# Inverse square roots by ScalarE's root and one Newton step, attention's loads issued by GpSimd, and a fifth float16 tile for p

## The chip, the cores and the metric

The kernel runs on one core of one Trainium2 chip. The metric is device time in microseconds (us) of one execution. The engines are TensorE (PE, matmuls; its weight loads are listed apart as PEld), VectorE (DVE), ScalarE (ACT), GpSimd (POOL) and SyncE (SP), which issues DMAs; each has its own instruction queue and works through it in order. "SPq" in a profile is the sync queue. A line number such as L810 is a line of the kernel before.

## The reference

For x of 1024 x 512, layer-normalised to xn, the output is `x + attention(xn) * silu(ffn(xn))`. Attention has 32 query heads and 8 key/value heads of width 128; q and k are normalised per head, `t * rsqrt(mean(t*t) + 1e-6) * w`, the scores get a causal mask and a bias `slope * (key position - query position)`, and after softmax and the product with v the heads go through Wo. The feed-forward network has 4-bit integer weights with a scale and a zero per group of 128, inner width 1792. Inputs and output are float32.

## The kernel before

The work runs in four stages that follow one another. **Feed-forward** (layer norm, gate and up, then down): its result, through silu, is stored to DRAM as `gd`. **Projections**: twelve, in the order kv, q, q, four times; a `Projection` object holds one. Each has eight tiles of 128 rows. In `tile` TensorE makes a tile in PSUM (four PSUM tiles rotate), ScalarE copies it to `f` and squares it with a row sum into `ss`, one column for each head. After four tiles (a half) `queue_half` puts the rest of the work into later steps of a clock that ticks once per tile: `inverse` makes `ms` on VectorE and a first guess of its inverse root by an integer shift and subtraction (`rsqrt_seed`), `newton` runs three times on GpSimd (at steps 0, 1 and 1), the last one for a q also multiplying by a scale for each head; `normalize` on GpSimd (step 2 on) multiplies `f`; `halves` on VectorE (step 4 on) splits it into two float16 halves; a DMA transposes these and another stores them to `kd` or `qd` in DRAM. Between the tiles `prepare` scales and splits the weights of the next projection: `split_head` casts to `wh` on ScalarE (L527), then VectorE makes `wl` (L528), which TensorE needs for the next projection's first tile. The last two projections run together with the first steps of attention, and the last one's finishing is spread over attention's steps.

**Attention** goes through 8 groups (a key head with its four query heads), each in four blocks of 256 query rows, each block in 4 heads x 2 row tiles: a `step` for each, 256 in all. Step n issues, for different steps of the pipeline, the scores of n (TensorE), the exponentials of n-1 (VectorE L799, ScalarE L800), the high float16 half of n-3's p (ScalarE, L810), the low half of n-4's (VectorE, L819) and the DMA transpose of both into `pT` (L820), the product with v nine steps later, and then the output projection. The pair of halves is a tile `p16`; P16_BUFS of them rotate, so L810 waits for the transpose that read the tile P16_BUFS uses before. A block's number of key columns runs from 256 to 1024, so the length of a step varies. The loads of attention (`load_keys`, `load_values`, `load_queries`, `load_wo`, and `gate_load` for the last sum) are issued by the sync queue, which also issues every transpose. `split_wo` makes a float32r pair of Wo's rows on ScalarE and GpSimd (L770), six steps ahead of use. `relative` makes the distance bias of a group from a constant tile `nrel` on GpSimd.

The order on each engine is that of the code: nothing is scheduled anew, and semaphores are put where data or buffers need them.

Of the kernel before, what the change touches and what calls it, by code (L numbers as in the profile page):

```python
# [10 lines left out]
F32 = mybir.dt.float32  # L11
# [10 lines left out]
P = 128  # L22
# [36 lines left out]
GATE_SUMS = [27, 28, 30, 31]  # L59
GATE_STEP = 2  # L60
PF_BUFS = 5
P16_BUFS = 4

_START = 2 ** (-(2 ** (-(math.log2(H) - 3))))
SLOPES = np.array([_START * _START**i for i in range(H)], dtype=np.float32)
# [5 lines left out]
def attention_gated_by_ffn_kernel(ctx, tc, x, gu_w, gu_z, gu_s, dn_w, dn_z, dn_s, wq, wkv, wo, qnw, knw, out):  # L71
# [47 lines left out]
    cs = const.tile([P, NH], F32, name="cs")  # L119
    rc = const.tile([P, 1], F32, name="rc")  # L120
    eps = const.tile([P, 3 * HKV // 2, NH], F32, name="eps")
    gsT = const.tile([P, NI, 2, KT], F32, name="gsT")

    kd = [dram.tile([P, 2, NT, 2 * HD], F16, name=f"kd{i}") for i in range(HKV // 2)]
# [339 lines left out]
    class Projection:  # L464
        def __init__(self, k, kind, i):
            self.k, self.kind, self.i, self.name = k, kind, i, f"{kind}{i}"
            self.n = NH if kind == "q" else 2
            self.f, self.ss, self.inv = {}, {}, {}

        def load(self, j):  # L470
            if j == 0:
                self.raw = wide.tile([P, KT, 512], F32, tag="wide", name=f"w{self.name}")
            sp.dma_start(self.raw[:, j], (wq if self.kind == "q" else wkv)[self.i, :, j])
# [13 lines left out]
        def norms(self):  # L487

            n = self.n
            pn = spare(self.k, f"n2_ps{self.k}")  # L490
            te.matmul(pn[:, 256 : 256 + n], lhsT=ones_bf, rhs=self.sb[:, :n], start=True, stop=True)
            if self.kind == "kv":
                for j in range(KT):
                    te.matmul(pn[:, :256], lhsT=ones_bf, rhs=self.sq[:, j, :], start=j == 0, stop=j == KT - 1)
            self.am = wp.tile([P, NH], F32, tag="am", name=f"am_{self.name}", bufs=2)[:, :n]
            ve.tensor_scalar(self.am, pn[:, 256 : 256 + n], 1.0 / W_SCALE**2, 1e-30, ALU.mult, ALU.max)
            rsqrt_seed(self.am, self.am)
            self.eps = eps[:, self.k, :n]
# [37 lines left out]
        def tile(self, t):  # L536
            n, half, r = self.n, t // HT, t % HT
            if r == 0:
                self.f[half] = fq.tile([P, HT, n, HD], F32, tag="f", name=f"f_{self.name}_{half}", bufs=3)
                self.ss[half] = fq.tile([P, HT, n], F32, tag="ss", name=f"ss_{self.name}_{half}", bufs=3)  # L540
                self.jk = wp.tile([P, NH, HD], BF16, tag="jk", name=f"jk_{self.name}_{half}")
            ps = ps1("o" if t % 2 else "m", f"ps_{self.name}_{t}")
            rows = slice(t * P, (t + 1) * P)
            for j in range(KT):
                mm3(ps, (xth[:, j, rows], xtl[:, j, rows]), (self.wh[:, j, :], self.wl[:, j, :]), j == 0, j == KT - 1)
            se.copy(self.f[half][:, r], ps[:, : n * HD].rearrange("p (g d) -> p g d", g=n))
            for i in range(n):
# [15 lines left out]
        def inverse(self, half):  # L563
# [156 lines left out]
    nrel = ap1.tile([P, S], F32, name="nrel", bufs=1)  # L720
    ge.iota(nrel, pattern=[[-1, S]], base=S - P, channel_multiplier=1, allow_small_or_imprecise_dtypes=True)
    ge.affine_select(nrel, nrel, pattern=[[-1, S]], compare_op=ALU.is_ge, fill=1e20, base=S - P, channel_multiplier=1)

    def queue_half(p, half):

# [20 lines left out]

    def load_keys(g):
        kT[g] = ap1.tile([P, NT, 2, P], F16, tag="kT", name=f"kT{g}")
        sp.dma_start(kT[g].rearrange("p t a k -> p t (a k)"), kd[g // 2][:, g % 2])

    def load_values(g):
        vT[g] = ap1.tile([P, NT, 2, HD], F16, tag="vT", name=f"vT{g}")
        sp.dma_start(vT[g].rearrange("p t a d -> p t (a d)"), vd[g])

    def load_queries(g, qb):
        qT[g, qb] = ap1.tile([P, NQT, 2, NH, P], F16, tag="qT", name=f"qT{g}_{qb}")
        sp.dma_start(
            qT[g, qb].rearrange("p t a g q -> p t (a g q)"), qd[g][qb * NQT : (qb + 1) * NQT].rearrange("t p c -> p t c")
        )

    def load_wo(g, i):
        wor[g, i] = late[0].tile([P, DM], F32, tag="wor", name=f"wor{g}_{i}", bufs=2)
        sp.dma_start(wor[g, i], wo[(g * NH + i) * HD : (g * NH + i + 1) * HD, :])

    def split_wo(g, i):
        woh[g, i] = late[0].tile([P, DM], F32R, tag="woh", name=f"woh{g}_{i}", bufs=5)
# [100 lines left out]
    def gate_load(b):  # L867
        g, qb = blocks[b]
        gx = fq.tile([P, 2, NQT, DM], F32, tag="f", name=f"gx{qb}", bufs=3)
        t0 = qb * NQT  # L870
        sp.dma_start(gx[:, 0], gd[t0 : t0 + NQT].rearrange("t p c -> p t c"))
        sp.dma_start(gx[:, 1], x[t0 * P : (t0 + NQT) * P, :].rearrange("(t p) c -> p t c", p=P))
        gates[b] = gx

    def gate_partial(b, i):
# [86 lines left out]
                act(w, r // 2)  # L962

    last_ps = None
    early = 0
    for k, p in enumerate(projections):
        if k == len(projections) - 3:
            load_keys(0)
            load_values(0)
            load_queries(*blocks[0])  # L970
            relative(0)
        for t in range(NT):
            prepare(k + 1, t)
            if t == NT - 1:
# [58 lines left out]
```

## Time and profile before

| | |
|---|---|
| median of 3 runs | 1084.39 us (1084.32 to 1085.37) |
| the profiled execution's own time | 1091.69 us |
| its span, first to last instruction | 1089.9 us |
| mean granted TensorE clock | 0.984 |
| PE busy | 1026.4 us, 94% |
| DVE busy | 887.6 us, 81% |
| ACT busy | 792.0 us, 73% |
| POOL busy | 415.9 us, 38% |
| DMA q1 (all DMAs of the sync queue) | 196.93 MB, 82.6% of 16 engines' span |

A line of the view of waits reads: engine, operand and line that waited, "<-" who ended the wait, us in total, times, longest. The chain of waits is followed back from the last instruction, at each step to what released it; its pieces are given as start, length, and what it was. The share of the DMA engines is a mean over 16. A busy TensorE is not TensorE at its peak, since matmuls overlap.

### The profile page before, as it was taken

What the parts mean: (1) busy time and instruction counts of PE and PEld (TensorE: products, weight loads), DVE (VectorE), ACT (ScalarE), POOL (GpSimd) and SP (SyncE); (2) the same over time, 40 slices, a digit from 0 to 9 for tenths busy, and PEclk for the clock granted to TensorE, in tenths of its full rate; (3) what the DMA queues carried; (4) which work ended last, traced back from release to release, by engine and by line L of the source; (5) the groups of instructions that cost most, each with busy time, mean ns of one, the idle gap of its engine ahead of it and who ended that gap; (6) DMA issues with size and microseconds to landing.
All of it is one profiled execution on the core that took longest, in us unless ns stands there. A gap on an engine that the chain in (4) does not pass through costs nothing.

```text
span 1089.9 us, 18604 instructions
## 1 busy us (share of the span) xinstructions
PE 1026.4 (94%) x5912; PEld 622.4 (57%) x5912; DVE 887.6 (81%) x1746; ACT 792.0 (73%) x2123; POOL 415.9 (38%) x551
## 2 busy tenths in 40 slices
PE   7899899999999898997999999999998999999986
PEld 4444378744444343445666666666665566666664
DVE  7888987448878888886898896998897878969974
ACT  5777633568786786787887796896886878868961
POOL 1588663137877878641105013023040030132222
PEclk8999999999999999998999999999999999999998
DMA  6123155237989999999989999998998999999993
GB/s 198 47 98 125 60 160 141 89 106 164 226 219 208 241 200 259 228 189 212 213 187 199 197 206 187 202 210 183 198 203 182 196 205 176 203 222 206 235 203 88
DMA packets 445888, 198.11 MB, mean 182 GB/s; under 512 B 394402, under 2 KB 403934, under 8 KB 445790
## 3 DMA queue, kind: packets, MB, share of 16 engines
q1 hardware_dynamic: 445790, 196.93, 82.6%
q8 instruction: 46, 0.75, 0.3%
q14 instruction: 52, 0.43, 0.2%
HBM read 71.03 MB, written 29.36 MB: 92 GB/s over the span
## 4 chain that ended last, share of the span: by engine, by line
PE 59%; DMA 13%; DVE 11%; ACT 8%; issue 5%; POOL 3%; SPq 1%; DVEq 0%; ACTq 0%; POOLq 0%
DMA pT<-p 12%; PE gu_ps L252 6%; PE av L108 4%; PE s L108 4%; PE s L109 4%; PE s L110 4%; PE av L109 4%; PE av L110 4%; PE ps_q L109 3%; PE ps_q L110 3%; PE op L110 3%; PE op L108 3%; PE ps_q L108 3%; PE op L109 3%; PE dn_ps L110 2%
## 5 line engine op out<-in xcount | busy, mean ns | idle before, releaser
L819 DVE SCALAR_TENSOR_TENSOR p<-pf,row,p 128x1024 f16<-128x1024 f32 (+7 forms) x256 | 216.6, 846 | 76.9 <-ACT p L810 74.8
L810 ACT ACTIVATE p<-pf,row 128x1024 f16<-128x1024 f32 (+7 forms) x256 | 197.0, 770 | 73.7 <-DMA pT<-p 70.2
L800 ACT ACTIVATE pf<-pf,row 128x1024 f32<-128x1024 f32 (+7 forms) x256 | 197.2, 770 | 38.5 <-DVE row L799 36.7
L770 POOL TENSOR_TENSOR wol<-wor,woh 128x512 fp32r<-128x512 f32 x32 | 59.8, 1870 | 429.5 <-ACT woh L769 373.6
L799 DVE CUSTOM_DVE_ANT_0 pf<-s,trel,cs 128x1024 f32<-128x1024 f32 (+7 forms) x256 | 207.5, 810 | 4.1 <-PE s L110 4.0
L108 PE MATMUL av<-pT,vT 128*128 128x256 f16 (+1 forms) x640 | 171.7, 268 | 25.2 <-DMA pT<-p 24.8
L109 PE MATMUL av<-pT,vT 128*128 128x256 f16 (+1 forms) x640 | 169.2, 264 | 0.0
L110 PE MATMUL av<-pT,vT 128*128 128x256 f16 (+1 forms) x640 | 169.0, 264 | 0.0
L108 PE MATMUL s<-kT,qT 128*128 128x512 f16 (+3 forms) x384 | 125.5, 327 | 6.6 <-DVE row L799 6.2
L109 PE MATMUL s<-kT,qT 128*128 128x512 f16 (+3 forms) x384 | 125.4, 327 | 0.0
L110 PE MATMUL s<-kT,qT 128*128 128x512 f16 (+3 forms) x384 | 123.8, 327 | 0.0
L108 PEld LDWEIGHTS <-vT 128*128 128x128 f16 x640 | 62.5, 98 | 106.9 <-issue 84.8
L108 PE MATMUL op<-woh,oh 128*128 128x512 f32 x248 | 121.7, 491 | 0.0
L109 PE MATMUL ps_q<-wl_q,xth 128*128 128x512 f16 x256 | 98.2, 383 | 6.7 <-DVE wl_q L528 6.7
L110 PE MATMUL op<-woh,ol 128*128 128x512 f32 x248 | 99.1, 400 | 0.0
L110 PE MATMUL ps_q<-wh_q,xtl 128*128 128x512 f16 x256 | 98.3, 384 | 0.0
L109 PE MATMUL op<-wol,oh 128*128 128x512 f32 x248 | 97.9, 395 | 0.4 <-POOL wol L770 0.4
L108 PE MATMUL ps_q<-wh_q,xth 128*128 128x512 f16 x256 | 98.2, 384 | 0.0
L847 ACT ACTIVATE oh<-av,rv 128x256 fp32r<-128x256 f32 x128 | 58.9, 460 | 24.9 <-PE av L110 24.4
L853 DVE SCALAR_TENSOR_TENSOR ol<-av,rv,oh 128x256 fp32r<-128x256 f32 x128 | 61.3, 479 | 13.6 <-ACT oh L847 13.5
L597 POOL TENSOR_TENSOR f_q<-f_q,inv_q 128x512 f32<-128x512 f32 x64 | 71.2, 1132 | 1.4
L109 PEld LDWEIGHTS <-vT 128*128 128x128 f16 x640 | 63.7, 100 | 12.2 <-issue 2.7
(179 smaller groups left out, 2315.1 us busy)
## 6 DMA issues: line engine op xcount, KB each, us to landing
qd<-tr_q SPq DMA_DIRECT2D x64, 256.0 KB, 3.6
qT<-qd SPq DMA_DIRECT2D x32, 512.0 KB, 4.4
wq<-in_wq SPq DMA_DIRECT2D x32, 256.0 KB, 3.9
wor<-in_wo SPq DMA_DIRECT2D x32, 256.0 KB, 3.7
gui<-in_gu_w SPq DMA_DIRECT2D x13, 512.0 KB, 3.6
wkv<-in_wkv SPq DMA_DIRECT2D x16, 256.0 KB, 3.8
vd<-v SPq DMA_DIRECT2D x8, 512.0 KB, 4.1
kd<-tr_kv SPq DMA_DIRECT2D x32, 128.0 KB, 2.5
```

The source lines that it names most:

```text
L108: te.matmul(ps, lhsT=lh, rhs=rh, start=first, stop=False)
L109: te.matmul(ps, lhsT=lh, rhs=rl, start=False, stop=False)
L110: te.matmul(ps, lhsT=ll, rhs=rh, start=False, stop=last)
L252: te.matmul(banks[j][:, k, :], lhsT=w[:, j, ws], rhs=x[:, j, k * 512 : k * 512 + 512], start=x is xth, stop=x is xtl)
L597: ge.tensor_tensor(f, f, ib, ALU.mult)
L770: ge.tensor_tensor(wol[g, i], raw, woh[g, i].bitcast(F32), ALU.subtract)
L799: ve.tensor_tensor_reduce(p, ps, trel[g][:, S - w :], cs[:, hh : hh + 1], 3e38, ALU.add, ALU.min, least[:, c])
L800: se.activation(p, p, AF.Exp, bias=least[:, c], scale=-1.0, accum_out=total[:, c])
L810: se.activation(p16[u, qt][:, :, 0, :], pf[u, qt], AF.Copy, scale=scale[:, qt : qt + 1])
L819: ve.scalar_tensor_tensor(lo, p, scale, hi, ALU.mult, ALU.subtract)
L847: se.activation(oh, av_ps[u], AF.Copy, scale=rv[:, g : g + 1])
L853: ve.scalar_tensor_tensor(ol, av_ps.pop(u), rv[:, g : g + 1], oh.bitcast(F32), ALU.mult, ALU.subtract)
```

## The change

Four edits:

- For the first ten projections the first guess and three Newton steps become ScalarE's square root of `ms` (at step 0, behind the next tile's squares in ScalarE's queue), a reciprocal on VectorE and one Newton step on GpSimd (both at step 1). The last two keep the guess and three steps. The q scale of each head is put into the squares instead (an immediate of the activation, and `steep` times `eps`), so the last Newton step has no form of its own.
- The loads of attention, 88 DMAs, are issued by GpSimd in place of the sync queue (the diff shows kT's; vT, qT, wor and the two of `gate_load` change in the same way).
- `p16` has five tiles in place of four.
- The constant `nrel` is gone: the first group's bias is made in its own tile, ahead of the projections, and each later one is scaled from the one before.

```diff
-P16_BUFS = 4
+P16_BUFS = 5
...
+    steep = const.tile([P, NH], F32, name="steep")
+    for i in range(NH):
+        ve.memset(steep[:, i : i + 1], (STEEPER[i] / Q_SCALE) ** 2)
...
+            self.by_root = k < 3 * HKV // 2 - 2
...
             ve.scalar_tensor_tensor(self.eps, self.am, 1e-6 * X_SCALE**2, self.am, ALU.mult, ALU.mult)
+            if self.kind == "q":
+                ve.tensor_tensor(self.eps, self.eps, steep, ALU.mult)
...
-                se.activation(self.jk[:, i], ps[:, i * HD : (i + 1) * HD], AF.Square, accum_out=self.ss[half][:, r, i : i + 1])
+                se.activation(
+                    self.jk[:, i],
+                    ps[:, i * HD : (i + 1) * HD],
+                    AF.Square,
+                    scale=STEEPER[i] / Q_SCALE if self.kind == "q" else 1.0,
+                    accum_out=self.ss[half][:, r, i : i + 1],
+                )
...
-            rsqrt_seed(a, y)
             self.inv[half] = (y, a, w)
-
-        def newton(self, half, last):
+            if self.by_root:
+                se.activation(y, a, AF.Sqrt)
+            else:
+                rsqrt_seed(a, y)
+
+        def newton(self, half, first):
             y, a, w = self.inv[half]
+            if first and self.by_root:
+                ve.reciprocal(y, y)
             ge.tensor_tensor(w, a, y, ALU.mult)
             ge.tensor_tensor(w, w, y, ALU.mult)
-            if last and self.kind == "q":
-                for i in range(NH):
-                    c = Q_SCALE / STEEPER[i]
-                    wi = w.rearrange("p (t g) -> p g t", g=NH)[:, i]
-                    ge.tensor_scalar(wi, wi, -0.5 * c, 1.5 * c, ALU.mult, ALU.add)
-            else:
-                ge.tensor_scalar(w, w, -0.5, 1.5, ALU.mult, ALU.add)
+            ge.tensor_scalar(w, w, -0.5, 1.5, ALU.mult, ALU.add)
             ge.tensor_tensor(y, y, w, ALU.mult)
...
-        for i in range(3):
-            due((i + 1) // 2, 0, lambda i=i: p.newton(half, i == 2))
+        if p.by_root:
+            due(1, 0, lambda: p.newton(half, True))
+        else:
+            for i in range(3):
+                due((i + 1) // 2, 0, lambda i=i: p.newton(half, i == 0))
...
-        sp.dma_start(kT[g].rearrange("p t a k -> p t (a k)"), kd[g // 2][:, g % 2])
+        ge.dma_start(kT[g].rearrange("p t a k -> p t (a k)"), kd[g // 2][:, g % 2])
...
-        trel[g] = ap1.tile([P, S], F32, tag="trel", name=f"trel{g}")
-        ge.tensor_scalar(trel[g], nrel, rc, float(SLOPES[g * NH + NH - 1]), ALU.mult, ALU.mult)
+        rel = trel[g] = ap1.tile([P, S], F32, tag="trel", name=f"trel{g}")
+        if g == 0:
+            ge.iota(rel, pattern=[[-1, S]], base=S - P, channel_multiplier=1, allow_small_or_imprecise_dtypes=True)
+            ge.affine_select(rel, rel, pattern=[[-1, S]], compare_op=ALU.is_ge, fill=1e20, base=S - P, channel_multiplier=1)
+            ge.tensor_scalar(rel, rel, rc, float(SLOPES[NH - 1]), ALU.mult, ALU.mult)
+        else:
+            ge.tensor_scalar(rel, trel[g - 1], float(SLOPES[g * NH + NH - 1] / SLOPES[g * NH - 1]), None, ALU.mult)
...
     last_ps = None
+    relative(0)
```

More of the change, by code (lines that the diff above doesn't have):

```diff
@@ L719, in attention_gated_by_ffn_kernel @@
     ap1 = ctx.enter_context(tc.tile_pool(name="attn1", bufs=2, side="right"))
-    nrel = ap1.tile([P, S], F32, name="nrel", bufs=1)
-    ge.iota(nrel, pattern=[[-1, S]], base=S - P, channel_multiplier=1, allow_small_or_imprecise_dtypes=True)
-    ge.affine_select(nrel, nrel, pattern=[[-1, S]], compare_op=ALU.is_ge, fill=1e20, base=S - P, channel_multiplier=1)
     def queue_half(p, half):
@@ L748, in load_keys @@
         kT[g] = ap1.tile([P, NT, 2, P], F16, tag="kT", name=f"kT{g}")
-        sp.dma_start(kT[g].rearrange("p t a k -> p t (a k)"), kd[g // 2][:, g % 2])
+        ge.dma_start(kT[g].rearrange("p t a k -> p t (a k)"), kd[g // 2][:, g % 2])
     def load_values(g):
         vT[g] = ap1.tile([P, NT, 2, HD], F16, tag="vT", name=f"vT{g}")
-        sp.dma_start(vT[g].rearrange("p t a d -> p t (a d)"), vd[g])
+        ge.dma_start(vT[g].rearrange("p t a d -> p t (a d)"), vd[g])
     def load_queries(g, qb):
         qT[g, qb] = ap1.tile([P, NQT, 2, NH, P], F16, tag="qT", name=f"qT{g}_{qb}")
-        sp.dma_start(
+        ge.dma_start(
             qT[g, qb].rearrange("p t a g q -> p t (a g q)"), qd[g][qb * NQT : (qb + 1) * NQT].rearrange("t p c -> p t c")
@@ L762, in load_wo @@
         wor[g, i] = late[0].tile([P, DM], F32, tag="wor", name=f"wor{g}_{i}", bufs=2)
-        sp.dma_start(wor[g, i], wo[(g * NH + i) * HD : (g * NH + i + 1) * HD, :])
+        ge.dma_start(wor[g, i], wo[(g * NH + i) * HD : (g * NH + i + 1) * HD, :])
     def split_wo(g, i):
@@ L870, in gate_load @@
         t0 = qb * NQT
-        sp.dma_start(gx[:, 0], gd[t0 : t0 + NQT].rearrange("t p c -> p t c"))
-        sp.dma_start(gx[:, 1], x[t0 * P : (t0 + NQT) * P, :].rearrange("(t p) c -> p t c", p=P))
+        ge.dma_start(gx[:, 0], gd[t0 : t0 + NQT].rearrange("t p c -> p t c"))
+        ge.dma_start(gx[:, 1], x[t0 * P : (t0 + NQT) * P, :].rearrange("(t p) c -> p t c", p=P))
         gates[b] = gx
@@ L970, in attention_gated_by_ffn_kernel @@
             load_queries(*blocks[0])
-            relative(0)
         for t in range(NT):
```

## The prediction

> **What bounds the kernel now.** I read the page's forty slices first, then busy time by stage, the waits, the chain of waits and the sync queue's own waits. In the slices each digit is a busy share in tenths.
>
> ```profile
> PE   7899899999999898997999999999998999999986
> ...
> PEclk8999999999999999998999999999999999999998
> DMA  6123155237989999999989999998998999999993
> ```
>
> TensorE is near full everywhere; the DMA engines are near full from the projections on. Stage by stage (in each line: length, busy us and instruction counts of TensorE, its weight loads, VectorE, ScalarE and GpSimd, then the granted clock, DMA share, GB/s):
>
> ```profile
> 240.00:480.00 240.00, 232.70 (x1080) 105.49 (x1078) 198.58 (x404) 181.72 (x821) 186.34 (x380) 0.99 0.94 215
> 480.00:515.00 35.00, 27.16 (x174) 17.05 (x173) 26.23 (x47) 27.15 (x69) 3.20 (x2) 0.92 1.09 214
> 515.00:1065.00 550.00, 527.04 (x3582) 358.69 (x3580) 469.44 (x1044) 436.39 (x988) 102.00 (x88) 1.00 0.99 200
> ```
>
> TensorE idles 7.3 us in the projections (240-480), 7.8 us in the hand-over (480-515) and 23.0 us in the attention proper (515-1065): 38 us within the change's reach. All else there is matmul work that the change leaves alone. Who waits (us in total, times, longest):
>
> ```profile
> ACT p L810 <- DMA pT<-p: 70.2, 53, 4.9
> ...
> PE av L108 <- DMA pT<-p: 24.8, 20, 3.4
> ...
> DVE q L609 <- POOL f_q L597: 22.4, 14, 2.9
> ...
> PE ps_q L109 <- DVE wl_q L528: 6.7, 3, 3.3
> ```
>
> Line 810 writes the float16 high half of p into one of four tiles, and waits until the transpose that read the tile four uses ago has landed. TensorE then waits for later transposes. The chain shows the loop closed (start, us, what):
>
> ```profile
> 497.29 0.74 ACT p L810
> 498.03 4.60 DMA pT<-p
> ...
> 502.65 0.94 ACT p L810
> ...
> 503.62 0.91 DVE p L819
> ...
> 505.33 5.20 DMA pT<-p
> ```
>
> In the projections GpSimd is late with the normalised q, VectorE waits behind it in order, its weight split (L528) comes late, and TensorE with it: 6.7 of the 7.3 us. The sync queue stands in front of the transposes with waits of its own for the loads' buffers:
>
> ```profile
> SPq L763 <- POOL wol L770: 12.9, 11, 2.2
> ...
> SPq L757 <- PE s L110: 4.1, 10, 0.7
> ```
>
> **What the Trainium skill says.** "DMA: Bandwidth & Descriptors", section "Issuing engines are not separate DMA queues": DMAs from any engine run on the same 16 DMA engines, and a second issuing engine saves only issue time. The DMA share of 0.99 in attention fits one shared resource; no GpSimd-issued DMA is in this trace. The same page, "Latency and other measured facts", puts the first byte at about 0.6 us from the sync queue and 1 us from GpSimd; not shown here. "SBUF — State Buffer", section "Who interferes with whom": a VectorE instruction with two SBUF inputs, or one in a two-port mode, contends with GpSimd's reads. The trace agrees: the cast at L609 takes 411 ns at its shortest and 683 on average over 64, the subtraction at L610 691 and 928; the slow ones (1.26 and 1.41 us) stand beside GpSimd's multiplies.
>
> **The change part by part.** *Newton steps.* Ten projections have 20 halves. A q half costs GpSimd now three times (438+296+344) ns, two times 389 and four times 328: 5.3 us. Afterwards one step: 438+296+344+389 = 1.5. A k half: 3 x (397+355+268+305) = 4.0, afterwards 1.3. With 12 q and 8 k halves GpSimd loses 12 x 3.8 + 8 x 2.7 = 67 of its 186 us in the stage, and the normalising starts some 3 us sooner. VectorE loses 40 seed instructions of 174 ns, gains 20 reciprocals (174 ns at L95) and a few [128,4] products: -3 us. Its excess from sharing, 64 x (683-411+928-691) ns = 33 us, should fall with GpSimd's work. ScalarE gains 20 roots (0.22 us at L93) and one table load (1.28 us there): 5.7 us on an engine that has 58 us free in the stage.
>
> The root adds a wait: ScalarE stands until VectorE has written ms (L569). Setting the end of the ScalarE group that precedes each root against the end of that ms, the 20 waits would be 0 to 5.7 us, 46 us in all, if VectorE stayed as late as it is. Behind it on ScalarE are the next tile's eviction and, in the first halves, the last weight cast (L527). Four PSUM tiles of 2.56 us each cover about 7 us of eviction; the cast has three tiles before TensorE needs it. So I cost the wait at nothing; the cover gone, it would cost what rival 2 says. VectorE, being relieved, should be less late too. I take -5 us for the stage. Bounds: +15 and -11 (all idle time, plus two stretches of 30 us granted 0.94 of the clock, 3.6 us).
>
> *The fifth tile.* 53 waits at L810 sum to 70.1 us. With a fifth tile each waits for a transpose one step earlier; steps come every 550/250 = 2.2 us. Taking 2 us off each wait leaves 11 us, taking 1.5 leaves 18: three quarters or more go. They go to TensorE's benefit only where the transpose was what TensorE lacked, and as far as the DMA engines (0.99) and VectorE (469 of 550 us) can follow. In some stalled stretches DMA share is lower (0.74, 0.74, 0.64 in the 5 us windows from 820), so there is room there: they are bound by the round trip of ScalarE, VectorE, queue and transpose (4.0 us median to landing).
>
> *Loads on GpSimd.* 88 loads (8 kT, 8 vT, 32 qT, 32 wor, 8 gx) leave the sync queue: about 0.57 us of issue each, 50 us in all, and the 12.9 + 4.1 us of waits shown, in front of transposes of 1.41 us each. Their bytes stay, so the engines' load does. On GpSimd each load passes wol's subtraction (L770) and the last projection's finishing; wol must be ready six steps ahead, kT, vT and qT are asked for several steps early. GpSimd is busy 102 of 550 us, so 88 loads at 1 us (my estimate from the skill's first-byte figure; bounds 0.57, as on the sync queue, and 4) are covered. If one delays a wol, TensorE waits as it did once (0.4 us): 8 places, at most 4 us. The last projection's eight normalisations (two in every fourth block of attention) stand behind a load, with two steps of slack. The iota moves, work unchanged: it waits for freed memory while GpSimd is idle (18.6 us). The memsets precede VectorE's wait for its first input: nothing. The q scale moves into an immediate: nothing.
>
> Fifth tile and loads share one answer: in attention -12 of 23 us (bounds 0 and -20), in the hand-over -5 of 7.8 idle and 2.8 of clock loss (0.92 over 35 us; bounds 0 and -9). The stall that is next is VectorE's own pace, 93% in full blocks, or the DMA engines.
>
> Sum: -5 - 12 - 5 = -22 us against the profiled execution's 1091.69 us (span 1089.9 and 1.8 around it), giving 1069.7. The median of the runs, 1084.39, lies 7.3 us below the profiled time; I carry the difference over: **1062 us**.
>
> **The rivals.** 1: *the DMA engines are already the bound.* For: 0.99 in attention, and the bytes stay. Against: of the eleven 5 us windows from 515 to 1065 in which TensorE idles over 0.75 us, five have 0.72 to 0.86 (the other six 0.96 to 1.27). Then attention and hand-over give 1 us each and the projections 5: 1077. 2: *the root's wait stays on the path*, slower. Place: ScalarE after the fifth tile of each projection and the first of the next; price 46 us; for it, VectorE is late by over 2.5 us in 9 of 20 halves; against, the PSUM cover of 7 us and the relief of GpSimd. With attention and hand-over still giving 17 and the projections nothing, it decides from 37% of 46 us passing through; at 60% the time is 1084 - 17 + 28 = 1095. 3: *a load holds GpSimd about 4 us*, so that the eight last q, and each wol beside them, come 4 us late: the gain in attention is lost, 1084 - 10 + 32 = 1106; from 1.5 us late each (12 us) it would eat that gain. 4: *everything opens*: idle time and clock both come back, -36: 1048.
>
> **How the numbers follow.** Forecast 0.58 (1054 to 1070), rival 1 0.20 (1070 to 1082), rival 4 0.10 (1044 to 1054), rivals 2 and 3 0.12. The range 1049 to 1082 leaves out half of rival 4 and the slow cases, under 0.2. 0.2% is 2.2 us, about what a measurement of this kernel can tell from no change: faster 0.86 (forecast, rival 1, rival 4, less 0.02), same 0.03, slower 0.11.
>
> **What would show it.** Right: L810's waits for the transposes under 25 us; TensorE's for pT under 12; no load among the sync queue's waits; GpSimd near 120 us busy in the projections; VectorE's waits for f_q under 10 us. Wrong: ScalarE waiting over 20 us for ms at the root with TensorE's projections stalled behind it; GpSimd's issues of several us; waits at L810 unchanged at a DMA share of 1.0. A forecast too small would show TensorE without idle time from 480 on.

## The result, and the profile after

The changed kernel takes **1100.18 us** (median of 4 runs, 1095.24 to 1104.17); the kernel before, beside it, 1084.88 us (4 runs, 1084.32 to 1086.26). The ratio is 1.0128, with a 95% interval of 1.0101 to 1.0154: slower by 1.3%, where 1062 us had been forecast. The profiled execution of the changed kernel took 1095.24 us (span 1093.4 us), the lowest of its times. The profiled execution of the kernel before took 1091.69 us, above all its timed runs. So the two profiles lie 3.6 us apart where the medians lie 15, and they show less of the loss than there is. Among the runs below, two of e12's six executions were slow ones (1.8 and 2.0% above its fastest) and are left out of its median and ratio.

The forty slices of the changed kernel, each digit a tenth:

```profile
PE   7899899999999999987899899998999999969996
...
PEclk9999999999999999998999999999999999989999
DMA  5124254237999989899989999899999999998993
```

TensorE dips to 6 in a slice near 970 us, where the kernel before had 9. The DMA share is as high as it was. By stage (length, busy us and instruction counts of TensorE, its weight loads, VectorE, ScalarE and GpSimd; clock, DMA share, GB/s):

```profile
240.00:480.00 240.00, 233.85 (x1096) 106.39 (x1095) 192.31 (x397) 185.28 (x838) 127.12 (x188) 1.00 0.95 218
480.00:515.00 35.00, 24.72 (x168) 16.53 (x167) 24.32 (x43) 27.29 (x73) 7.80 (x9) 0.90 1.15 219
515.00:1065.00 550.00, 524.02 (x3550) 357.73 (x3548) 474.53 (x1031) 435.12 (x980) 154.74 (x156) 0.98 1.01 197
```

TensorE idles 6.2 us in the projections (7.3 before), 10.3 in the hand-over (7.8) and 26.0 in attention (23.0). Attention's granted clock is 0.98 where it was 1.00. GpSimd is busy 59 us less in the projections. The waits of the changed kernel (in total, times, longest):

```profile
POOL qT L769 <- PE s L110: 231.1, 20, 21.7
...
ACT oh L864 <- PE av L110: 66.8, 64, 7.5
...
PE av L108 <- DMA pT<-p: 31.6, 16, 8.1
ACT p L827 <- DMA pT<-p: 27.5, 17, 7.4
...
ACT inv_q L592 <- DVE ms_q L582: 8.0, 7, 2.4
...
ACT inv_kv L592 <- DVE ms_kv L582: 7.3, 4, 2.6
...
DVE q L621 <- POOL f_q L609: 4.9, 4, 1.7
```

Line 827 is the old L810, and its wait for the transposes has fallen from 70.2 to 27.5 us. TensorE's wait for them has risen from 24.8 to 31.6, with one of 8.1 us. GpSimd stands 231 us at qT's buffer. The queues of the changed kernel (packets, MB, share of the 16 engines):

```profile
q1 hardware_dynamic: 427998, 159.17, 71.1%
q0 software_dynamic: 10624, 37.75, 12.6%
```

The kernel before had all its loads on q1:

```profile
q1 hardware_dynamic: 445790, 196.93, 82.6%
```

The longest stall lies at the turn to the last group. GpSimd's timeline there (start, us, what), and TensorE's instruction that ends the stall, its wait in brackets:

```profile
961.12 0.73 POOL L888 DMA_DIRECT2D gx<-gd  x1
961.85 0.72 POOL L889 DMA_DIRECT2D gx<-in_x  x1
...
965.32 0.59 POOL L761 DMA_DIRECT2D kT<-kd  x1
967.94 0.71 POOL L769 DMA_DIRECT2D qT<-qd  x1 [2.02 <-PE s L110]
968.64 0.72 POOL L888 DMA_DIRECT2D gx<-gd  x1
969.35 0.70 POOL L889 DMA_DIRECT2D gx<-in_x  x1
970.05 0.57 POOL L765 DMA_DIRECT2D vT<-vd  x1
```

```profile
975.72 0.37 PE L108 MATMUL av<-pT,vT 128*128 128x256 f16 x1 [8.09 <-DMA pT<-p]
```

And the same stretch in steps of 4 us (columns as above):

```profile
962.00:966.00 4.00, 3.72 (x33) 2.80 (x32) 2.88 (x9) 2.46 (x8) 3.89 (x3) 1.00 1.30 179
966.00:970.00 4.00, 1.64 (x13) 1.01 (x11) 1.38 (x5) 0.95 (x4) 2.06 (x3) 0.95 1.22 180
970.00:974.00 4.00, 0.00 (x0) 0.00 (x0) 0.00 (x0) 0.00 (x0) 0.62 (x2) 0.50 1.06 380
974.00:978.00 4.00, 2.28 (x10) 1.71 (x11) 0.35 (x1) 0.89 (x3) 0.00 (x0) 0.50 1.06 353
```

TensorE stands still from 967.6 to 975.7 us. The seven loads in the timeline are 3.5 MB, and from 970 on the engines move 350 to 380 GB/s. The largest time from issue to landing of a transpose of p is 16.3 us, where it was 7.4. TensorE's clock falls to 0.50 from 970 on. Five more half-speed stretches of 3.4 us each begin at 495, 509, 536, 615 and 676 us, each within a stall of 2.5 to 3.7 us or less than 1 us after its end. The kernel before has two such stretches between 480 and 1065 us, 10 us in all; the changed kernel has 27 us.

The Trainium skill ("TensorE: Matmul & The Clock Gate", section "Part 1: The HAM clock gate") says that about 3.4 us of idling throttles TensorE to half rate until it has been busy for as long again. The lengths fit: every stretch in these profiles after 480 us but the one that ends with the kernel is 3.4 us or a multiple of it. The idling that sets one off was often shorter here: 2.5 us (to 676.1) and 3.0 us (to 536.7) in the changed kernel, 2.3 us in the kernel before (to 672.5), while another stall there, of 3.3 us (to 1047.5), brought none.

### The profile page after: what moved, and what is told of

It reads as the page before. It is cut to its first block, busy times and chain, and to the rows that moved or that the text cites. A ratio compares the mean times of both kernels' runs of the same rounds, so it can differ in the third digit from the quotient of the medians.

```text
span 1093.4 us, 18429 instructions
## 1 busy us (share of the span) xinstructions
PE 1024.7 (94%) x5912; PEld 624.5 (57%) x5912; DVE 889.3 (81%) x1738; ACT 797.6 (73%) x2144; POOL 418.9 (38%) x431
## 3 DMA queue, kind: packets, MB, share of 16 engines
q0 software_dynamic: 10624, 37.75, 12.6%
## 4 chain that ended last, share of the span: by engine, by line
PE 57%; DVE 13%; DMA 11%; ACT 9%; issue 7%; POOL 2%; SPq 0%; DVEq 0%; POOLq 0%; ACTq 0%
DMA pT<-p 10%; PE gu_ps L255 6%; PE av L108 4%; PE av L110 4%; PE av L109 4%; PE s L108 3%; PE s L109 3%; PE s L110 3%; PE op L108 3%; PE op L110 3%; PE op L109 3%; PE ps_q L108 3%; PE ps_q L110 3%; PE ps_q L109 3%; DVE pf L816 2%
## 5 line engine op out<-in xcount | busy, mean ns | idle before, releaser
L836 DVE SCALAR_TENSOR_TENSOR p<-pf,row,p 128x1024 f16<-128x1024 f32 (+7 forms) x256 | 223.4, 873 | 41.6 <-ACT p L827 39.0
L816 DVE CUSTOM_DVE_ANT_0 pf<-s,trel,cs 128x1024 f32<-128x1024 f32 (+7 forms) x256 | 207.4, 810 | 23.8 <-PE s L110 22.9
L827 ACT ACTIVATE p<-pf,row 128x1024 f16<-128x1024 f32 (+7 forms) x256 | 196.7, 769 | 31.5 <-DMA pT<-p 27.5
L108 PE MATMUL av<-pT,vT 128*128 128x256 f16 (+1 forms) x640 | 172.8, 270 | 31.6 <-DMA pT<-p 31.6
L108 PEld LDWEIGHTS <-vT 128*128 128x128 f16 x640 | 62.9, 98 | 112.7 <-issue 94.0
L769 POOL DMA_DIRECT2D qT<-qd x32 | 23.4, 732 | 231.3 <-PE s L110 231.1
L870 DVE SCALAR_TENSOR_TENSOR ol<-av,rv,oh 128x256 fp32r<-128x256 f32 x128 | 61.2, 478 | 24.1 <-ACT oh L864 23.7
L609 POOL TENSOR_TENSOR f_q<-f_q,inv_q 128x512 f32<-128x512 f32 x64 | 76.2, 1215 | 1.4
```

The source lines that it names most:

```text
L108: te.matmul(ps, lhsT=lh, rhs=rh, start=first, stop=False)
L609: ge.tensor_tensor(f, f, ib, ALU.mult)
L816: ve.tensor_tensor_reduce(p, ps, trel[g][:, S - w :], cs[:, hh : hh + 1], 3e38, ALU.add, ALU.min, least[:, c])
L827: se.activation(p16[u, qt][:, :, 0, :], pf[u, qt], AF.Copy, scale=scale[:, qt : qt + 1])
L836: ve.scalar_tensor_tensor(lo, p, scale, hi, ALU.mult, ALU.subtract)
L870: ve.scalar_tensor_tensor(ol, av_ps.pop(u), rv[:, g : g + 1], oh.bitcast(F32), ALU.mult, ALU.subtract)
```

## The experiments

All are compared with the kernel before, run on the same chip beside them. The last column is worked out from the packet records of the traces. From 480 us to the end the durations of all DMA packets are added and divided by 16 engines; those of up to 256 bytes, nearly all from transposes, stand apart from the rest. A duration is not only the moving of bytes: packets of 4 KB took from 159 ns to 4.1 us in e9, and the trace does not part off what of it is waiting. Since packets overlap, the sum can exceed the time. And 480 us is a fixed point: a kernel that is later there has more left to move. From e16 to e8 that is 8,800 small packets, about 13 us of the sum; between e1 and the changed kernel it is 1,500, about 2 us.

```
kernel                              median us   ratio to before (95%)      packet time after 480 us: small + rest = sum
before                                 --         1                         447 + 145 = 592
changed kernel                      1100.18     1.0128 (1.0101-1.0154)     456 + 149 = 605
e1  all loads on sync               1077.87     0.9929 (0.9906-0.9953)     444 + 140 = 584
e2  only the loads on GpSimd        1131.96     1.0411 (1.0367-1.0455)     476 + 153 = 629
e3  only root and one Newton step   1079.17     0.9941 (0.9922-0.9961)     450 + 137 = 587
e4  only the fifth tile             1080.20     0.9961 (0.9942-0.9980)     456 + 139 = 595
e5  kT vT qT gx on ScalarE          1098.68     1.0110 (1.0082-1.0137)     454 + 144 = 599
e6  gx on sync                      1090.64     1.0032 (1.0014-1.0050)     445 + 151 = 597
e7  only wor on GpSimd              1076.20     0.9890 (0.9862-0.9919)     447 + 145 = 592
e8  rows of 512 bytes               1131.54     1.0398 (1.0366-1.0431)     490 + 170 = 660
e9  paced by VectorE                1103.74     1.0148 (1.0105-1.0192)     473 + 151 = 624
e10 pairs back to back on sync      1089.85     1.0031 (1.0019-1.0043)     443 + 138 = 581
e11 four tiles                      1103.03     1.0172 (1.0137-1.0207)     458 + 149 = 607
e12 loads after landing             1112.63     1.0227 (1.0191-1.0263)     482 + 149 = 631
e13 paced, gx on sync               1098.12     1.0087 (1.0054-1.0119)     467 + 150 = 617
e14 e7 with values ten steps behind 1073.64     0.9890 (0.9859-0.9921)     448 + 146 = 594
e15 qT and wor on GpSimd            1094.80     1.0073 (1.0046-1.0100)     456 + 148 = 605
e16 e7 less 30 loads of wor         1062.70     0.9787 (0.9767-0.9807)     452 + 109 = 561
```

My first theory was that the loads on a queue of their own make the transposes late, above all when GpSimd issues several back to back. The rivals were that the fifth tile puts too many transposes in flight, and that the root costs.

### One part at a time (e1 to e4)

e1 is the changed kernel with all 88 loads on sync; e2, e3 and e4 are the kernel before with one of the three parts (e4 with the new distances too, which make room for the tile). The edit of e1, in each of six places, and e4's first line:

```diff
-        ge.dma_start(kT[g].rearrange("p t a k -> p t (a k)"), kd[g // 2][:, g % 2])
+        sp.dma_start(kT[g].rearrange("p t a k -> p t (a k)"), kd[g // 2][:, g % 2])
...
-P16_BUFS = 4
+P16_BUFS = 5
```

> The changed kernel with its 88 loads back on the sync queue (one Newton step and five tiles stay). Theory (the loads' own queue makes the transposes land late): 1062 to 1075 us, TensorE's waits for pT at most 15 us, the slowest transpose of attention under 8 us. Rival A (the fifth tile puts too many transposes in flight): still 1090 to 1105, TensorE's waits for pT stay near 30 us. Rival B (the root or the new trel is what costs): still 1095 to 1105.

> The kernel before with only the 88 loads issued by GpSimd (four tiles, three Newton steps). Theory: slower than before, 1095 to 1112 us, with transposes of over 10 us and TensorE's waits for pT over 30 us. Rival A (fifth tile): about 1084, since the fifth tile is missing. Rival B (root): about 1080.

> The kernel before with only the root and the single Newton step. Theory: 1078 to 1082 us (3 to 6 us less, in the projections). Rival B (the wait for the root's input stays on the path): 1090 or more.

> The kernel before with only the fifth float16 pair of tiles (and the distances kept in one buffer, which makes room for it). Theory: 1070 to 1078 us, waits of the high half for the transposes under 25 us. Rival A (too many transposes in flight): 1090 or more, TensorE's waits for pT near 30 us.

The loads alone cost 4.1%. Root and fifth tile each gain 0.4 to 0.6%, and both together (e1) 0.7%. Both rivals fall. e1's median lies 3 us above the band that the theory gave it, e4's 2 us and e2's 20 us above their own; and TensorE's waits for pT in e1, put at 15 us at most, are 25.7. The waits of e1:

```profile
ACT oh L864 <- PE av L110: 56.8, 56, 4.3
...
ACT p L827 <- DMA pT<-p: 27.1, 21, 3.3
PE av L108 <- DMA pT<-p: 25.7, 19, 2.8
```

L827 waits as little as in the changed kernel (27.1 us), but no wait of TensorE for pT exceeds 2.8 us, and the slowest transpose lands after 7.2 us. TensorE's sum (25.7) stays at the old 24.8, and while ScalarE waits 43 us less at L827, it waits 32 us more for the product with v (56.8 us, 24.4 before). The tile alone is worth about 5 us (e4). What the loads on GpSimd add to the changed kernel lies in long stalls of TensorE: after 480 us it has seven of over 2 us, 27.5 us in sum (six of them, 24.2 us, for a pT), where e1 has four, 9.4 us in sum. The shorter waits are fewer than in e1.

### Which queue, which loads, which rows (e5 to e8)

e5 issues kT, vT, qT and gx from ScalarE; e6 puts only gx back on sync; e7 puts all but wor back. e8 leaves gaps of 64 bytes in the DRAM scratch, so that kT, vT and qT move in rows of 512 bytes:

```diff
-        ge.dma_start(vT[g].rearrange("p t a d -> p t (a d)"), vd[g])
+        se.dma_start(vT[g].rearrange("p t a d -> p t (a d)"), vd[g])            # e5
+        ge.dma_start(vT[g].rearrange("p t a d -> p t (a d)"), vd[g][:, :, : 2 * HD])   # e8
...
-    vd = [dram.tile([P, NT, 2 * HD], F16, name=f"vd{g}") for g in range(HKV)]
+    vd = [dram.tile([P, NT, 2 * HD + 32], F16, name=f"vd{g}") for g in range(HKV)]     # e8
```

> The changed kernel with the loads of kT, vT, qT and gx (56) issued by ScalarE instead of GpSimd; wor stays on GpSimd. Theory 1 (any queue of its own lets the loads' large packets run beside the transposes and starve them): 1090 to 1110, transposes over 8 us stay, and ScalarE's 56 issues cost something besides. Theory 2 (only GpSimd's software queue does this): 1078 to 1086, the slowest transpose under 8 us.

> The changed kernel with only the 8 loads of gx back on the sync queue. Theory (a stall is as long as the bytes that GpSimd issues back to back; 967 us has qT, two gx and vT, 2 MB): the 8 us stall goes to 3 to 4 us and its clock loss shrinks, 1088 to 1096; stalls of 2.5 to 4 us behind the pairs qT and vT stay. If gx alone is the cause: 1078 to 1082. If gx does not matter: 1098 to 1102.

> The changed kernel with only the 32 loads of wor on GpSimd, kT, vT, qT and gx back on the sync queue. Theory (bursts of 1 MB and more do it, wor comes alone with 256 KB): 1076 to 1082, about the kernel with all loads on the sync queue (1078). If each load on GpSimd hurts the transposes by itself: 1085 to 1092.

> The changed kernel with gaps of 64 bytes in the DRAM scratch of kT, vT and qT, so that their loads (and qT's stores) move rows of 512 bytes instead of rows of 2 KB and more; qT is loaded by two DMAs. Theory (the DMA engines take turns packet by packet, so a queue of large packets takes most of the time): the stalls behind pairs of qT and vT shrink to 0 to 1.5 us, 1084 to 1093; the stall with gx stays at 4 us or more. Rival (the engines' time is shared by queue or by bytes, or 512-byte rows only cost more): stalls unchanged or longer, 1100 to 1115.

e5 costs nearly as much as the changed kernel, with a stall of 7.5 us in the hand-over and two of over 6 us in attention. So it isn't GpSimd's kind of queue alone. Part of it may be ScalarE's time for 56 issues, which this run does not part off. ScalarE's queue cut most of these loads into packets of 2 KB, as the sync queue does, and GpSimd's into 4 KB; so the size of the packets isn't what all of this turns on. gx makes up about 10 of the 22 us between the changed kernel and e1; e6's time lies in the band of the theory of piles, but its longest stall, to 978.5 us, is 5.7 us where 3 to 4 were expected. wor on GpSimd costs nothing, and e7 is as fast as e1 or a little faster (the intervals overlap). e8 is slower than either theory had put it, and it didn't try what it was meant to. Its queues (packets, MB, share):

```profile
q1 hardware_dynamic: 459742, 159.17, 72.9%
q0 software_dynamic: 11136, 37.76, 13.8%
```

GpSimd's packets stayed at 3.4 KB on average, where kT, vT and qT in packets of 512 bytes would be 49,000 of them; only the stores on q1 got smaller (31,744 packets more than in the changed kernel), and TensorE's idle time in the projections rose to 11.0 us. The packets of over 2 KB took 272 ns each against the changed kernel's 242. So rows of 512 bytes cost time even in packets of 4 KB, and whether small packets would spare the transposes was not tried.

### Piles and overtaking (e9 to e13, e15)

In the changed kernel GpSimd waits at qT's buffer, and what has queued up goes out 0.7 us behind qT: vT six times, gx once, and wor thirteen times. e9 puts a copy ahead of each of these loads, which keeps GpSimd in step; e13 is e9 with gx on sync. e12 copies from the last pT instead, so that the load goes only when that transpose has landed:

```diff
+    def pace():
+        if at_step[0] is not None:
+            u, qt = at_step[0]
+            ge.tensor_copy(tick, rows16[u][0][:, qt : qt + 1])              # e9, e13
+            ge.tensor_copy(tick, pT[u][:, 0, 0, qt * P : qt * P + 1])       # e12
...
     def load_keys(g):
         kT[g] = ap1.tile([P, NT, 2, P], F16, tag="kT", name=f"kT{g}")
+        pace()
         ge.dma_start(kT[g].rearrange("p t a k -> p t (a k)"), kd[g // 2][:, g % 2])
...
+        at_step[0] = at(n - 2)             # e9, e13; n - NQT - 3 in e12
```

e10 makes piles on the sync queue (e1 with the edit below), e11 is the changed kernel with P16_BUFS = 4, and e15 has only qT and wor on GpSimd.

```diff
-            if qt == 0 and hh == 3 and g + 1 < HKV:
+            if qt == 0 and hh == 1 and g + 1 < HKV:      # e10: kT or vT right behind qT
```

> The changed kernel with each of the 56 loads of kT, vT, qT and gx on GpSimd preceded by a copy of one column that VectorE wrote in the step before, so that GpSimd can't run ahead of the steps and the loads go out spread as on the sync queue. Theory 1 (the bursts do it: GpSimd stands at qT's buffer, then issues what has piled up behind): 1074 to 1082, no stall over 3 us after 515. Theory 2 (a second queue of large packets does it by itself, whenever the load goes): 1092 to 1102, stalls of 3 us and more behind single loads stay.

> All 88 loads on the sync queue, with kT and vT of the next group asked for in the same step as the next qT instead of four steps later, so that 1 MB goes out back to back there 14 times. Theory 1 (bursts do it, on any queue): 1084 to 1092, stalls of 2 to 4 us at those 14 places. Theory 2 (a queue beside the transposes' own does it): 1076 to 1080, as with the loads on the sync queue four steps apart.

> The changed kernel with four float16 pairs of tiles instead of five (root and GpSimd's loads stay). If the fifth tile is what takes up most of a late transpose, so that the same loads cost more without it: 1115 to 1130. If it only adds its own 2 to 5 us: 1102 to 1106.

> The changed kernel with a copy of one column of pT on GpSimd ahead of each load of kT, vT, qT and gx, so that the load goes out only when the last transpose issued in program order has landed. Theory A (loads on a queue of their own overtake the transposes that on the sync queue stand ahead of them): 1076 to 1084, no stall over 3.5 us, the 967 us one included. Theory B (two queues at once slow the transposes, whichever started first): 1090 to 1104, the stall beside the gx loads stays over 5 us.

> Pacing by VectorE's last column as in the run paced before, but with gx on the sync queue. It is the kernel with gx on sync (1090.6) plus pacing. Theory (piles of kT, qT and vT make the stalls of 2.5 to 4 us): 1078 to 1085. If the piles do not matter: 1088 to 1094.

> The changed kernel with qT and wor on GpSimd, kT, vT and gx on the sync queue: loads of 512 KB, but not piled with others except for wor. Theory (piles): 1076 to 1084. If each load of 512 KB that overtakes the transposes costs by itself: 1086 to 1094.

Pairs of the 512 KB loads as the main cause on GpSimd's queue fall. e9 spread these as meant: kT, qT and vT went out 6 to 10 us apart (wor still followed thirteen of the qT after 0.7 us, in e13 too). The stalls between 515 and 900 us were then at most 2.6 us, but the kernel took 1103.74, and e13 took 1098.12 where the same loads without pacing (e6) took 1090.64. Nor does it come from the copies' holding GpSimd up: in both runs TensorE waits only 0.5 us for wol in all, and for no load. Both runs lie above the bands of either theory, by 2 and 4 us. e15 cost 17 us over e1, but it is no test of single loads: with kT and vT on the sync queue, nine of its qT after 500 us went out within 0.8 us of one of these, and thirteen had a wor behind them. Its 1094.80 us are 0.8 above the band of the second theory. The place of the longest stall, in e9 (4 us each; columns as above):

```profile
961.00:965.00 4.00, 3.43 (x28) 2.40 (x27) 2.57 (x9) 2.26 (x8) 3.97 (x4) 1.00 1.29 196
965.00:969.00 4.00, 2.37 (x22) 1.67 (x19) 2.10 (x8) 1.46 (x5) 0.69 (x3) 1.00 1.62 92
969.00:973.00 4.00, 0.00 (x0) 0.00 (x0) 0.00 (x0) 0.00 (x0) 0.00 (x0) 0.74 0.77 88
973.00:977.00 4.00, 0.00 (x0) 0.00 (x0) 0.00 (x0) 0.00 (x0) 0.00 (x0) 0.50 1.14 295
```

Only gx, gx and kT, 1.5 MB, were issued between 960.7 and 965.1 us. Yet from 965 to 973 the DMA share was 1.62 and 0.77 at 92 and 88 GB/s, and most of the loads' bytes passed only from 973 on. In e1, where the same three loads went out at 960.7, 961.3 and 964.4 us on the sync queue, the engines moved twice as much and TensorE never stopped:

```profile
966.00:970.00 4.00, 4.00 (x27) 2.46 (x25) 3.04 (x7) 3.13 (x10) 1.53 (x2) 1.00 0.90 202
970.00:974.00 4.00, 4.00 (x24) 2.60 (x23) 3.65 (x12) 3.31 (x10) 2.38 (x2) 1.00 0.78 193
```

e12 doesn't save it either: waiting until the last transpose had landed makes 1112.63 us, above the bands of both theories. This run isn't clean. The gate holds GpSimd back so long that wol comes late for TensorE:

```profile
POOL tick L765 <- DMA pT<-p: 330.6, 45, 16.5
...
PEld op L109 <- POOL wol L793: 8.4, 6, 2.2
...
PE op L109 <- POOL wol L793: 6.5, 6, 1.9
```

These waits make up 15 us, on the matmuls and weight loads of one engine that partly overlap. Less these 15 us it would still be at 1098 (an estimate), so e12 speaks against the 1076 to 1084 of the overtaking theory, but less firmly than e9 and e13 speak against the pairs.

e10 shows that piles do cost on the sync queue, 12 us over e1, by another way: its packet time is the lowest but one, and TensorE stalls for pT 2.3 to 3.1 us behind five of the pairs of qT and kT. The sync queue at one such place (start, us, what), and TensorE's instruction after the stall:

```profile
958.64 0.98 SPq L769 DMA_DIRECT2D qT<-qd  x1
959.66 0.47 SPq L761 DMA_DIRECT2D kT<-kd  x1
960.24 7.76 SPq L837 DMA_TRANSPOSE pT<-p  x2
```

```profile
970.24 0.27 PE L108 MATMUL av<-pT,vT 128*128 128x256 f16 x1 [3.13 <-DMA pT<-p]
```

qT and kT go out together, ahead of the next transposes.

e11 shows that the fifth tile is worth 3 us beside GpSimd's loads (the intervals overlap). e2 and e11 both have four tiles and GpSimd's loads; e11 has the root and the new distances as well, and is 29 us faster. By the first loads of wor (496.7 and 488.1 us) 8.6 us of it have come about, in the projections. The other 20 arise in attention, where the two differ only in the instruction that makes the distances. It goes with a packet time of 629 against 607 us and one stall of 20 us in e2 against 12 in e11; why the same loads go so differently was not settled.

### What goes with the time, and a test of it (e14, e16)

Over the profiled executions of all eighteen kernels, packet time after 480 us and total time have a correlation of 0.89. That alone proves little, since the sum is 0.96 to 1.02 of the time after 480 us in every kernel, and single runs break it: e7 has 8 us more packet time than e1 and isn't slower, e10 has 4 us less and is 12 us slower. The packets are the same in number and size in all but e8 and e16, apart from the loads being cut into fewer and larger ones on GpSimd's queue: 10624 for 37.75 MB, about 3.6 KB each, against the 17792 packets, 2.1 KB each, by which q1 shrank. What differs is what each takes. The loads' own packets take 58 to 60 ns per KB in the kernels that load qT from GpSimd (66 in e8) and 53 to 57 in those that load it on sync. For the small packets the two groups overlap. One that starts while no packet of 2 KB or more is in flight takes 20.5 to 21.3 ns in all eighteen kernels. Beside a packet of a load it takes 28 to 32 ns where qT is loaded on sync (29 in e1, 31.5 in e4) and 28 to 35 where it comes from GpSimd (31 in the changed kernel, 38 in e8).

So the 21 us between e1 and the changed kernel (584 and 605) lie elsewhere than beside the loads, as far as small packets go: 9 us are in the loads' own packets, 2 in small ones that e1 had moved before 480 us. The small ones that start beside a load sum to 63 us in the changed kernel and 64 in e1. Those that start while a packet of the instruction queues (q8 and q14) is in flight sum to 50 and 38; what makes that difference is not known, and over the eighteen kernels it goes from 38 to 55. In the paced e9 and e13 more does lie beside the loads (79 and 74 us).

The records also show how two queues share the engines. In the half microseconds in which GpSimd's loads moved over 240 GB/s (some 150 of them in the changed kernel), about one small packet went beside one of the loads: 1.1 to 1, and from 0.7 (e11) to 1.4 (e13) in the other kernels that load qT from there. One for one in number is about one to fourteen in bytes: the transposes move some 20 KB per us there and 141 otherwise. While the 3.5 MB pass, a transpose of up to 512 KB hardly advances, and that is most of the stall of 8 us. But on the sync queue a load holds the transposes up as well (15 KB per us in e1 while loads move as fast), so this sharing alone doesn't yield the 22 us.

e16 tests whether the DMA engines' time sets the end. It takes bytes away on a queue where issuing them cost nothing: e7 with only the first two loads of wor, whose tiles serve all heads. e14 is e7 with the product with v ten steps behind.

```diff
-        wor[g, i] = late[0].tile([P, DM], F32, tag="wor", name=f"wor{g}_{i}", bufs=2)
+        if g or i > 1:
+            wor[g, i] = kept[i % 2]
+            return
+        wor[g, i] = kept[i] = late[0].tile([P, DM], F32, tag=f"wor{i}", name=f"wor{g}_{i}", bufs=1)
...
-AV_LAG = 9
+AV_LAG = 10      # e14
```

> The version with only wor on GpSimd (1076.2), with 30 of the 32 loads of wor left out: the first two tiles serve for all heads (part of the output projection's weights is therefore not the reference's; the work on them is the same). 7.9 MB at 57 ns per KB on 16 engines are 27 us of the DMA engines' time. Theory (the DMA engines' time sets attention's end, with TensorE idle for 29 us after 480): 1052 to 1066. Rival (the packet time only goes along with something else, such as the order of the transposes): 1073 to 1079.

> The version with only wor on GpSimd (1076.2), with values ten steps behind scores instead of nine, so each transpose has one more step (2.2 us) to land. If TensorE's waits for pT (24.5 us there) are what is left: 1060 to 1070, those waits under 12 us. If the transposes only finish later by as much (DMA engines full, tiles of p given back no sooner): 1074 to 1080.

e16 takes 31 us of packet time away and 13.5 us of the kernel's (1062.70 against e7's 1076.20, whose ratios to before don't overlap). TensorE's and ScalarE's waits for the transposes, first e7, then e16:

```profile
PE av L108 <- DMA pT<-p: 24.5, 20, 3.2
ACT p L827 <- DMA pT<-p: 24.5, 22, 2.6
```

```profile
ACT p L832 <- DMA pT<-p: 16.2, 16, 2.3
...
PE av L108 <- DMA pT<-p: 13.3, 13, 2.7
```

24.5 became 13.3 us, and 24.5 became 16.2. So the DMA engines' time does set part of the end; the rest meets TensorE's own work, which filled 515 of the 525 us from 515 to 1040 us in e16. e14 brought nothing that can be told from e7 (0.9890 both; its 1073.64 us are 0.4 under the band of the second reading). TensorE's waits for pT fell nearly as far there, from 24.5 to 14.8 us, but ScalarE's at L827 rose from 24.5 to 44.6: with the same bytes to move, more time to land only moved the wait. e1, e7 and e14 beat both the changed kernel and the one before; e7's 1076.20 us is 0.9890 of the time before.

## Why the prediction was wrong

**The step that failed is in the loads' part, one sentence: "Their bytes stay, so the engines' load does."** It priced the move as issue time and as GpSimd's lateness, and put at nothing what loads on a second queue do to the transposes, since the bytes stay. They cost 22 us beside the other edits (1100.18 against e1's 1077.87) and 4.1% alone (e2), where they were to help. The bytes stayed and the engines' load did not: over the whole run, at the same bytes, the packets took 920 us of 16 engines' time in the changed kernel and 901 in e1, which differs only in the issuing queue. The kernel felt it as transposes that land late: at most 16.3 us from issue to landing against 7.2.

How the loss reaches the end can be followed in the two profiles, 16.1 us of span apart. From 480 us to the end TensorE idles 9.6 us more (45.8 against 36.2: the long stalls grew by 18 us, the shorter waits fell by 8), and it works at half speed for 22.9 us in place of 10.2, which costs half of the difference, 6.4 us. That the packets' sum rose too is shown, that this rise is what makes the transposes late is not: e7's sum is 8 us above e1's at no cost. By what mechanism a second queue delays them stays open.

*Loads, the other steps.* An issue on GpSimd was put at 1 us, bounds 0.57 and 4: the profile has 0.55 to 0.79 (the 1 us came from a figure for the first byte, which is not the issue's own time). No load is left among the sync queue's waits, as promised. A late wol cost nothing to speak of. But of the issue time saved on sync nothing shows: e1, with all 50 us of it back, is the faster kernel. Only wor, on GpSimd in e7, may have given a little (1 to 2 us, within the intervals).

*Newton steps.* Forecast -5 us; e3 measured -6 (1079.17 against 1085.28). In the changed kernel the transposes of p begin at 466.2 us instead of 470.5. GpSimd fell by 59 us (67 forecast) to 127, VectorE's wait for f_q from 22.4 to 4.9 us, and ScalarE waits 15.3 us for ms where 46 had been feared if VectorE stayed as late; VectorE itself lost 6.3 us where 3 were forecast. Only the place differs: idle time in the stage fell by a mere 1.2 us, and some 3.4 us came from two half-speed stretches of TensorE, at 366 and 434 us before, that are gone in this profile (e5, e12 and e13, with the same root, have one at 430 to 435). So the size of the gain came in part by luck. The 46 us of rival 2 didn't pass through.

*Fifth tile.* L827's wait fell to 27.5 us, against 11 to 18 forecast and 25 promised, and to 28.8 in e4; TensorE's waits for pT, promised under 12, are at 31.6. The mechanism was right, the size off: tile and loads together were to give 12 us in attention and 5 in the hand-over, and the tile alone gave 5 in all (e4), since TensorE's waits for pT stayed at 23.7. That wait is the term that was mis-sized. The fifth tile did not touch it; fewer bytes to move cut it to 13.3 (e16).

*The rivals.* Rival 1, the DMA engines already the bound, had 0.20; it was nearest to what bounds the kernel, and e16 shows it in part. I held against it five windows of 5 us with a share of 0.72 to 0.86, of eleven in which TensorE idles over 0.75 us. There are twelve; the other seven go from 0.96 to 1.39. The mean of 0.99 over 550 us was the better sign, though no proof: the share counts packets that overlap and reached 1.62 in e9. Even rival 1 put the kernel at 1077 (e1's time), since it too took the load as fixed. Rival 3 had the right sign, but its mechanism, a load that holds GpSimd for 4 us, is not there.

*What a page said of the issuing queue.* The Trainium skill, "DMA: Bandwidth & Descriptors", section "Issuing engines are not separate DMA queues", says that a second issuing engine saves only issue time. I read it as "costs nothing" as well, which it doesn't say. The same page, section "Queues, rings and completion order", says that each DMA engine takes turns between the queues it has work for, a whole packet at a time. The counts of about one small packet for one large fit it, if a packet of the trace is what the page calls one. That the load would then be no dearer in sum is what I had assumed, and what the runs contradict. Why the packets take longer in sum was not settled: there are stretches, like 965 to 973 us in e9, in which packets are in flight and neither queue moves much, and nothing tried here says what holds them.

## What to carry to other kernels

Where transposes by DMA are on the path, a load that shares the engines with them isn't free to move: large loads moved from the transposes' queue to another cost 22 us here at the same bytes. In the transposes' own queue, singly and spread among them, those of 512 KB cost least, and in pairs they cost 12 us more (e10). A buffer or a step of slack added in front of such a transpose moves the wait and gives a fraction of it (e4), or nothing (e14); fewer bytes gave 13.5 us (e16). And a stall of 2 to 4 us on TensorE can bring 3.4 us of half clock with it, up to 1.7 us more: it did with all five of that length between 480 and 1065 us in the changed kernel.

## What the runs showed of the hardware that was not expected

- Small packets (up to 256 bytes, nearly all of transposes) take 20.5 to 21.3 ns alone and 28 to 35 ns beside packets of loads, on whichever queue the loads are (38 in e8). Those of over 150 ns are 1.6% of those beside loads in the kernel before, 3.6% in the changed kernel and 4.7% in e12.
- Packets of the instruction queues hold the transposes up far more. Thirty of 16 KB and 27 to 29 of 8 KB pass after 480 us in every kernel, and small packets that start while one is in flight take 50 to 65 ns on average. From 0.5 to 1.25 us after one of 16 KB has started, the small packets that start in a quarter of a microsecond are 30 in the changed kernel, where they are 165 before it and from 2 us on. None of the experiments changed this.
- 32 loads of 256 KB on GpSimd's queue cost nothing (e7); 32 of 512 KB more (e15) cost 17 to 19 us, nine of them within 0.8 us of a load on the sync queue. What makes the difference, size, source or place, was not tried.
- Two queues with work share the DMA engines about one packet for one, where one has packets of 256 bytes and the other of 4 KB (0.7 to 1.4): some 20 KB per us for the first and 320 GB/s for the second in the changed kernel. Beside ScalarE's packets, most of 2 KB, it was 0.65 to 1 (e5).
- With both queues in use, the DMA share was about 1.2 on average at 90 GB/s for 8 us (e9), where 200 is usual.
- GpSimd's queue put eight rows of 512 bytes into a packet (e8), so rows don't set the size of its packets.
- On GpSimd a multiplication of 128x1024 float32 by one immediate takes 2.78 us; the one before, by a column and an immediate, takes 1.16.
